# First panel's scores: left sides multiplied from SBUF, pairs made one ahead, a bar on transposes and a higher rate of handed-out work

## The chip, the cores and the metric

The kernel runs on one core of a Trainium2 chip. The metric is the device time of one execution in microseconds. The kernel before takes 3166.89 us (median of four runs, 3164.97 to 3167.02). Engines are named as in the profile: PE is TensorE (matmul), DVE is VectorE, ACT is ScalarE, POOL is GpSimd, SP is SyncE, which issues most loads. "Stage" below means the first panel's scores: from the start of their first matmul to the start of the first matmul of the next projection, both read from the matmul timeline.

## The reference

Two graph attention layers on x (2708 x 1024) and an adjacency matrix. Only the first layer's scores matter here:

```python
h = jnp.maximum(_layernorm(x, axis=-1), 0.0)
f = h @ Wf + bf
g = h @ Wg + bg
e = jax.nn.relu(f @ g.T)
scores = jnp.where(adj > 0, e, NEG)
attention = jax.nn.softmax(scores, axis=1)
```

## The kernel before

The 2708 rows are cut into five panels of columns and, on the other side, into ten pairs of row tiles and a left-over. Products use a scheme with seven products M1 to M7 per pair in place of eight. Scores of a panel are computed pair by pair, q = 0 to 9. The left sides of a pair (transposed rows and four sums of them) are made once, kept in DRAM, and read back for every panel. Pairs 0 to 4 are made in earlier stages, beside other matmuls; pairs 5 to 9 are made inside the first panel's scores.

Making a pair is a list of pieces, each with a weight in microseconds. `behind(us)` adds credit and runs pieces while there is credit; `make_until(q)` runs pieces until pair q is complete, whatever the credit:

```python
    def behind(us, psum_free=False):
        credit[0] = min(credit[0] + us, 2 * us)
        while later and credit[0] > 0 and (psum_free or not later[0][3]) and (not later[0][4] or later[0][4]()):
            credit[0] -= one()
    ...
        put_norms = lambda q: put(4.2, lambda: norms(q), lambda: fetch(q))     # normalizing: VectorE, ScalarE
        put_rows = lambda q: put(0.5, lambda: rows(q))                          # row sums: GpSimd, and stores
    ...
            if i + 1 < len(todo):
                put_norms(todo[i + 1])                    # the pair after
            put_rows(q)
            put(0.5, lambda q=q: transposes(q), takes_psum=True)   # PE, ScalarE copies
            if i > 1:
                put_dots(q)                                         # VectorE
            put(2.7 if q != LEFT else 0.0, lambda q=q: last(q))     # four sums on VectorE, stores to DRAM
```

The scores of a pair (shortened). VectorE keeps program order here (`nc.hold`), so a piece handed out at some `behind` stands in VectorE's queue at exactly that place:

```python
        for q in range(NQ):
            make_until(q + 2)
            ...
            product(q, M1, X, True);  m1 = X + rb (two additions)
            left_over()     # M4 of the pair before, its eviction, mask, maximum, and behind(rate)
            product(q, M6, Z, True);  st_lo = Z + m1;  behind(rate)
            product(q, M5, Y, True);  st_hi = Y + m1;  negate the next mask;  behind(rate)
            product(q, M2, X, False); Sa_lo = X + rb;  behind(rate)
            product(q, M7, Z, False); Sb_hi = Z + st_hi;  behind(rate)     # fifth product: needs st_lo read
            product(q, M3, Y, False); Sa_hi = Y + st_lo; mask, maximum; transposes of the next mask
            behind(2 * rate)
```

M7 accumulates into the bank that M6 left, so it can't start before VectorE has done the addition st_lo. The pool `strm` holds twelve streaming buffers (left sides, adjacency blocks, row sums and others); the pool of PSUM has eight banks.

Of the kernel before, what the change touches and what calls it, by code (L numbers as in the profile page):

```python
# [18 lines left out]
P = 128  # L19
# [38 lines left out]
def kernel(  # L58
# [19 lines left out]
    nc = InOrder(tc)  # L78
# [30 lines left out]
    NQ = len(pairs)  # L109
    pair_of = {t: (t // 2, t % 2) for t in range(MONO)}  # L110
    LEFT = NQ
# [32 lines left out]
    def bank(name, shape=(P, W), dt=FP):  # L144
        return psum.tile(list(shape), dt, tag="bank", name=name)
# [39 lines left out]
    def put(us, go, fetch=None, takes_psum=False, ready=None):  # L185
        later.append([us, fetch, go, takes_psum, ready])

    def one():
        for it in later[:2]:
            if it[1]:  # L190
                it[1]()
                it[1] = None
        us, _, go = later.pop(0)[:3]
        go()
        return us
# [5 lines that stand above are left out]
# [25 lines left out]
    def row_halves(name, from_stream=False):  # L226
        return halves(stream(name)) if from_stream else [slot(name)[:, :W] for _ in range(2)]
# [14 lines left out]
    def add(o, a, b):  # L242
        nc.vector.tensor_tensor(o, a, b, OP.add)
# [7 lines left out]
    def load_rows_of(t, o, a):  # L251

        for e in range(2):
            if t == TINY:
                nc.gpsimd.memset(o[e], 0.0)
            for ps, r in places[t]:
                load(o[e][ps], a[r:r + ps.stop - ps.start, e * W:(e + 1) * W])
# [57 lines left out]
    c0 = consts.tile([P, 1], FP, name="c0")  # L315
    r_ = consts.tile([P, NCOL], FP, name="r")
    vb = [None, None]
    made, turned_tiles = set(), set()

    def make_pairs():  # L320
        xs, hT = {}, {}

        def fetch(q):
            xs[q] = []
            for t in units[q]:
                xs[q].append(row_halves("x"))
                load_rows_of(t, xs[q][-1], x)

        def norms(q):
            for k in range(2):  # L330
                normalize(xs[q][k])

        def rows(q):
            left_h(0, *xs[q]) if q == LEFT else pair_h(0, q, *xs[q])

        def turned(q, k, e):
            t = units[q][k]
            ps = bank("h_ps", (P, NH, P))
            for c in range(NH):
                nc.tensor.transpose(ps[:, c, :], xs[q][k][e][:, c * P:(c + 1) * P], ident)  # L340
            for i, (s, n) in enumerate(pieces[0]):
                if s == t:
                    o = first_h[e].rearrange("p (c i) -> p c i", c=NH)[:, :, i * P:i * P + n]
                    nc.vector.tensor_copy(o, ps[:, :, :n])
            return ps

        def transposes(q):
            if q == LEFT:
                two = stream("hsl", (P, 2, NH, P))
                for e in range(2):  # L350
                    nc.scalar.copy(two[:, e], turned(q, 0, e))
                    nc.scalar.copy(tinyT[:, e], turned(q, 1, e)[:, :, :B32])
                store(hsl_d.rearrange("p e c j -> p (e c j)"), two.rearrange("p e c j -> p (e c j)"))
            else:
                ts = [stream("hsT", (P, 2, NH, P)) for _ in range(4)]
                hT[q] = ts, lambda i: ts[i // 2][:, i % 2]
                for k, e, i in ((0, 0, 0), (0, 1, 3), (1, 0, 7), (1, 1, 6)):
                    nc.scalar.copy(hT[q][1](i), turned(q, k, e))
            turned_tiles.update(units[q])

        def sums(q):
            if q == LEFT:
                return
            ts, i = hT.pop(q)
            at = {m: i(k) for k, m in enumerate(BY_SCORES)}
            add(at[M5], i(7), at[M4])
            sub(at[M6], at[M5], at[M1])
            sub(at[M7], at[M1], i(7))
            sub(at[M3], at[M2], at[M6])
            for g, t in enumerate(ts):  # L370
                store(hs_d[q][:, 2 * g:2 * g + 2].rearrange("p m c j -> p (m c j)"), t.rearrange("p m c j -> p (m c j)"))

        def dots(q):
            for k, t in enumerate(units[q]):
                c = col_of[t]
                dot(r_[:, c:c + 1], xs[q][k], [vb[e][:, :W] for e in range(2)], c0)
                if t == MONO:
                    nc.gpsimd.dma_start(r_[:NM, HALF:HALF + 1], r_[NM:, c:c + 1])

        def drop(q, what):  # L380
            seen.setdefault(q, set()).add(what)
            if len(seen[q]) == 2:
                xs.pop(q)

        def last(q):
            sums(q)
            drop(q, "sums")
            made.add(q)

        def bias(q):  # L390
            dots(q)
            drop(q, "dots")

        seen = {}
        put_norms = lambda q: put(4.2, lambda: norms(q), lambda: fetch(q))
        put_rows = lambda q: put(0.5, lambda: rows(q))
        put_dots = lambda q: put(3.2, lambda: bias(q), ready=lambda: vb[0] is not None)
        todo = [0, 1, LEFT] + list(range(2, NQ))
        put_norms(todo[0])
        for i, q in enumerate(todo):  # L400
            if i + 1 < len(todo):
                put_norms(todo[i + 1])
            put_rows(q)
            put(0.5, lambda q=q: transposes(q), takes_psum=True)
            if i > 1:
                put_dots(q)
            put(2.7 if q != LEFT else 0.0, lambda q=q: last(q))
            if i == 1:
                put_dots(todo[0])
                put_dots(todo[1])  # L410

    def make_until(q):
        while min(q, NQ - 1) not in made:
            one()
# [615 lines left out]
    def scores(p, B):  # L1030
# [6 lines left out]
        spread(rb, columns_of(p, r_[:, first_col[p]:]))  # L1037
        acc = slot("acc")
        S = [None] * NT
        rate = (0.6, 1.0, 0.65, 0.65, 0.65)[p]  # L1040
        lefts = {}

        def product(q, m, ps, start):
            n, i = P, BY_SCORES.index(m)
            if i % 2 == 0:
                t = stream("As", (P, 2, NH, P))
                lefts[q] = t
                k = min(2, 7 - i)
                load(t[:, :k].rearrange("p m c j -> p (m c j)"),
                     hs_d[q][:, i:i + k].rearrange("p m c j -> p (m c j)"))  # L1050
            for c in range(NH):
                nc.tensor.matmul(ps[:n, :h], lefts[q][:, i % 2, c, :n], B[m][c // 2][:, c % 2, :h],  # L1052
                                 start=(start and c == 0), stop=(c == NH - 1), skip_group_check=True)
# [12 lines left out]
        def last(q, sb, Z, m1):  # L1066

            n = P
            product(q, M4, Z, False)
            add(sb[:n, lo], Z[:n, :h], m1[:n, lo])  # L1070
            finish(q, sb, 1)
            mk_sb.pop((p, q))
            behind(rate, True)

        nc.hold = True
        left_over = None
        for q in range(NQ):
            n = P
            make_until(q + 2)
            if q + 2 <= LEFT:  # L1080
                fetch(q + 2)
            sa, sb = slot("Sa"), slot("Sb")
            S[pairs[q][0]], S[pairs[q][1]] = sa, sb
            X, Y, Z = (bank(f"s{k}") for k in "xyz")
            m1, t = slot("sm1"), slot("st")
            product(q, M1, X, True)
            for s in (lo, hi):
                add(m1[:n, s], X[:n, :h], rb[:n, s])
            if left_over:
                left_over()  # L1090
            product(q, M6, Z, True)
            add(t[:n, lo], Z[:n, :h], m1[:n, hi])
            behind(rate, True)
            product(q, M5, Y, True)
            add(t[:n, hi], Y[:n, :h], m1[:n, hi])
            if q + 1 <= LEFT:
                convert(q + 1)
            behind(rate, True)
            product(q, M2, X, False)
            add(sa[:n, lo], X[:n, :h], rb[:n, lo])  # L1100
            behind(rate, True)
            product(q, M7, Z, False)
            add(sb[:n, hi], Z[:n, :h], t[:n, hi])
            behind(rate, True)
            product(q, M3, Y, False)
            add(sa[:n, hi], Y[:n, :h], t[:n, lo])
            finish(q, sa, 0)
            if q + 1 <= LEFT:
                turn(q + 1)
            behind(2 * rate, True)  # L1110
            left_over = lambda q=q, sb=sb, Z=Z, m1=m1: last(q, sb, Z, m1)
# [358 lines left out]
```

## Time and profile before

| | before |
|---|---|
| time, median | 3166.89 us |
| span of the profiled run | 3160.3 us |
| stage (203.32 to 384.91 us) | 181.6 us |
| stage with no wait at all (worked out in the prediction) | 163.7 us |
| from the stage's end to the sums of the first aggregation (384.91 to 549.34) | 164.4 us |
| from those sums (549.34) to the end | 2611.0 us |

In what follows, "the rest" is that last part.

The view of waits, asked for the matmul engine and the stage alone (us in total, times, longest), gives for the kernel before:

```profile
PE sz L1052 <- DVE st L45: 3.2, 2, 3.0
PE sy L1052 <- DVE st L45: 3.1, 2, 1.9
PE sx L1052 <- DMA As<-hs_d: 3.1, 1, 3.1
PE mk_ps L700 <- DVE nm L45: 2.2, 1, 2.2
```

That is 11.6 us of pauses. The other 6.3 of the 17.9 us over the wait-free stage are mostly matmuls that ran slowly after a pause (3.62, 3.46, 3.29 and 4.66 us in place of 2.10, 2.10, 2.10 and 4.04), and the restarts themselves.

### The profile page before, as it was taken

The page shows a single profiled execution, that of the slowest core. Times are in us where ns is not written, and L with a number is a line of the kernel's source. Part 1 is how long each engine was busy: PE and PEld are TensorE (multiplying, and loading weights), DVE is VectorE, ACT ScalarE, POOL GpSimd, SP SyncE. Part 2 cuts the span into 40 slices and gives each one's busy share as a digit, 9 for nine tenths or more (in the row PEclk, how much of TensorE's full clock was granted, in tenths as well). Part 3 has the DMA queues.
Part 4 walks back from the last instruction along what each step waited for, and adds up shares of the span by engine and source line. Part 5 has one row for each costly group of instructions (what it writes and reads, how often), then busy time and mean ns, then how long its engine had stood idle before and what let it go on. Part 6 is the DMA issues. An engine that isn't in the chain of part 4 may idle for free.

```text
span 3160.3 us, 36134 instructions
## 1 busy us (share of the span) xinstructions
PE 3085.6 (98%) x13218; PEld 2290.2 (72%) x13218; DVE 1768.6 (56%) x3561; ACT 505.2 (16%) x872; POOL 411.8 (13%) x552
## 2 busy tenths in 40 slices
PE   8999999999999999999999999997999999999998
PEld 5577777667876688876888885864767758678684
DVE  7758576375722666327771357658574471744612
ACT  3412020010200112001020002203131130211200
POOL 3624002210002100033000101020000000100000
PEclk9999999999999999999999999998999999999999
DMA  7858749676446675467845567596655465565655
GB/s 273 317 194 297 267 136 346 197 250 212 142 126 188 221 249 172 146 196 241 274 154 152 169 206 225 199 302 208 201 177 177 153 206 151 172 194 177 212 157 196
DMA packets 273497, 650.47 MB, mean 206 GB/s; under 512 B 38160, under 2 KB 105720, under 8 KB 273320
## 3 DMA queue, kind: packets, MB, share of 16 engines
q1 hardware_dynamic: 232296, 524.04, 51.8%
q0 software_dynamic: 41024, 124.12, 11.3%
q8 instruction: 105, 1.72, 0.2%
q14 instruction: 72, 0.59, 0.1%
HBM read 535.37 MB, written 112.67 MB: 205 GB/s over the span
## 4 chain that ended last, share of the span: by engine, by line
PE 87%; issue 6%; DVE 3%; POOL 1%; DMA 1%; ACT 0%; SPq 0%; POOLq 0%; DVEq 0%; ACTq 0%
PE gy L545 12%; PE gz L545 11%; PE gx L545 11%; PE sz L1052 7%; PE pz L948 5%; PE sy L1052 5%; PE sx L1052 5%; PE gv L545 5%; PE px L948 3%; PE M_ps L465 3%; PE qz L545 3%; PE py L948 3%; PE qy L545 2%; PE qx L545 2%; PE po L921 1%
## 5 line engine op out<-in xcount | busy, mean ns | idle before, releaser
L1052 PE MATMUL sz<-B,As 128*128 128x288 f32 (+2 forms) x1200 | 296.7, 397 | 3.2 <-DVE st L45 3.2
L1052 PEld LDWEIGHTS sz<-B,As 128*128 128x128 f32 x1200 | 230.3, 193 | 51.1 <-DVE st L45 4.2
L856 POOL TENSOR_TENSOR gT<-gT,rr 128x2304 f32<-128x2304 f32 (+5 forms) x20 | 75.4, 3769 | 1088.4 <-DVE rr L45 1003.1
L1052 PE MATMUL sx<-B,As 128*128 128x288 f32 (+2 forms) x800 | 203.1, 397 | 3.2 <-DMA As<-hs_d 3.1
L1052 PE MATMUL sy<-B,As 128*128 128x288 f32 (+2 forms) x800 | 199.1, 392 | 3.1 <-DVE st L45 3.1
L545 PE MATMUL gz<-P,hc 128*128 128x288 f32 (+2 forms) x800 | 186.0, 393 | 2.3 <-ACT gT L845 2.3
L545 PE MATMUL gz<-Sa,hc 128*128 128x288 f32 (+2 forms) x800 | 186.0, 393 | 2.3 <-ACT gT L845 2.3
L545 PE MATMUL gx<-P,hc 128*128 128x288 f32 (+2 forms) x800 | 185.6, 394 | 0.0
L545 PE MATMUL gy<-T,hc 128*128 128x288 f32 (+2 forms) x800 | 184.2, 391 | 0.0
L545 PEld LDWEIGHTS gz<-Sa,hc 128*128 128x128 f32 x800 | 151.2, 190 | 36.0 <-ACT gT L845 4.4
L545 PEld LDWEIGHTS gz<-P,hc 128*128 128x128 f32 x800 | 150.9, 190 | 35.6 <-ACT gT L845 4.4
L1052 PEld LDWEIGHTS sy<-B,As 128*128 128x128 f32 x800 | 151.7, 190 | 34.2 <-DVE st L45 4.1
L545 PEld LDWEIGHTS gx<-P,hc 128*128 128x128 f32 x800 | 152.8, 191 | 32.6 <-issue 1.9
L545 PEld LDWEIGHTS gy<-T,hc 128*128 128x128 f32 x800 | 152.0, 190 | 30.5
L1052 PEld LDWEIGHTS sx<-B,As 128*128 128x128 f32 x800 | 149.1, 190 | 32.2 <-issue 3.7
L701 ACT COPY mask<-mk_ps 128x1024 bf16<-128x1024 bf16 x55 | 55.6, 1011 | 623.9 <-PE mk_ps L700 320.9
L948 PE MATMUL px<-w,gT 128*128 128x512 f32 x320 | 144.3, 603 | 6.3 <-issue 5.8
L948 PE MATMUL py<-w,ps 128*128 128x512 f32 x320 | 143.4, 598 | 0.0
L948 PE MATMUL pz<-w,ps 128*128 128x512 f32 x320 | 141.8, 593 | 0.0
L948 PEld LDWEIGHTS px<-w,gT 128*128 128x128 f32 x320 | 60.5, 192 | 82.8 <-issue 80.0
L45 DVE TENSOR_TENSOR gT<-gy,u 128x288 f32<-128x288 f32 (+2 forms) x40 | 14.8, 433 | 183.5 <-PE gy L815 183.5
L948 PEld LDWEIGHTS py<-w,ps 128*128 128x128 f32 x320 | 60.9, 192 | 76.2 <-issue 72.7
(326 smaller groups left out, 5064.6 us busy)
## 6 DMA issues: line engine op xcount, KB each, us to landing
hc<-hg_d SPq DMA_DIRECT2D x350, 512.0 KB
As<-hs_d SPq DMA_DIRECT2D x150, 512.0 KB
w<-wt_d SPq DMA_DIRECT2D x96, 512.0 KB
w<-in_L_gnn_W_dram SPq DMA_DIRECT2D x72, 512.0 KB
md<-md_d SPq DMA_DIRECT2D x56, 512.0 KB
adj_i<-in_adj_dram SPq DMA_DIRECT2D x50, 512.0 KB
hg_d<-g POOLq DMA_DIRECT2D x40, 512.0 KB, 4.8
hs_d<-hsT POOLq DMA_DIRECT2D x40, 512.0 KB, 5.4
```

The lines of the kernel that those rows point to most:

```text
L45: i = f(*a, **k)
L465: nc.tensor.matmul(ps, wfT[a][c // NH][:, c % NH, :], wgT[b][c], start=(c == 0), stop=(c == NC - 1))
L545: nc.tensor.matmul(ps[d], left(m, k, d), right(m, k), start=(start and k == 0), stop=(k == K - 1 and m not in more), skip_group_check=True)
L701: nc.scalar.copy(mk[:, :, :k4 * P], ps[:, :, :k4 * P])
L856: nc.gpsimd.tensor_tensor(of(e, s), of(e, s), by(s, k), OP.mult)
L921: nc.tensor.matmul(ps, carry[:, e, k], w_[k], start=(start and k == 0), stop=(k == NH - 1), skip_group_check=True)
L948: nc.tensor.matmul(ps, left[i][m][:, k, :], w_[k], start=(start and k == 0), stop=(k == NH - 1), skip_group_check=True)
L1052: nc.tensor.matmul(ps[:n, :h], lefts[q][:, i % 2, c, :n], B[m][c // 2][:, c % 2, :h], start=(start and c == 0), stop=(c == NH - 1), skip_g ...
```

## The change

Its intent: pairs made inside the stage need not go through DRAM for the first panel, so their left sides are multiplied straight from the tiles in SBUF; each then holds four streaming buffers, so pairs are made only one ahead; and the making is handed out between products at a higher rate.

```diff
@@ make_pairs, sums
             ts, i = hT.pop(q)
+            if in_scores[0]:
+                fresh[q] = ts
@@ make_pairs, list of pieces
-            put(0.5, lambda q=q: transposes(q), takes_psum=True)
+            put(0.5, lambda q=q: transposes(q), takes_psum=True,
+                ready=lambda q=q: not in_scores[0] or q == LEFT or q <= now[0] + 1)
@@ scores, product
-            if i % 2 == 0:
+            if q in fresh:
+                lefts[q] = fresh[q][i // 2]
+            elif i % 2 == 0:
                 t = stream("As", (P, 2, NH, P))
@@ scores, end of left_over
             mk_sb.pop((p, q))
+            fresh.pop(q, None)
             behind(rate, True)
@@ scores, loop over q
-            n = P
-            make_until(q + 2)
+            n, now[0] = P, q
+            make_until(q + 1)
+            rate = 1.7 if NQ - 1 not in made else rates[p]
```

The rates of the panels stay (0.6, 1.0, 0.65, 0.65, 0.65). Cut here is where `in_scores`, `now` and `fresh` are set up; `in_scores[0]` turns true at the start of the stage.

More of the change, by code (lines that the diff above doesn't have):

```diff
@@ L317 @@
     vb = [None, None]
+    in_scores, now = [False], [0]
     made, turned_tiles = set(), set()
+    fresh = {}
     def make_pairs():
@@ L1039, in scores @@
         S = [None] * NT
-        rate = (0.6, 1.0, 0.65, 0.65, 0.65)[p]
+        rates = (0.6, 1.0, 0.65, 0.65, 0.65)
         lefts = {}
@@ L1072, in last @@
             mk_sb.pop((p, q))
+            fresh.pop(q, None)
             behind(rate, True)
-        nc.hold = True
+        nc.hold = in_scores[0] = True
         left_over = None
         for q in range(NQ):
-            n = P
-            make_until(q + 2)
+            n, now[0] = P, q
+            make_until(q + 1)
+            rate = 1.7 if NQ - 1 not in made else rates[p]
             if q + 2 <= LEFT:
```

## The prediction

> **What bounds the kernel now.** I read the page first, then the matmul timeline of the first 700 us, then the stretches of the stage that the change touches, and last the timelines of VectorE and GpSimd in that stage.
>
> ```profile
> PE 3085.6 (98%) x13218; PEld 2290.2 (72%) x13218; DVE 1768.6 (56%) x3561; ACT 505.2 (16%) x872; POOL 411.8 (13%) x552
> ```
>
> The matmul engine is busy for 3085.6 of 3160.3 us, so all its idle time is 74.7 us, 2.4% of the span. The change removes no matmul. It can only win back idle time, and only in the first panel's scores, which the matmul timeline places at 203.3 to 384.9 us (181.6 us). Ten pairs of row tiles (q = 0 to 9) are multiplied there, seven products each, and a tail. Pairs 0 to 4 were made before; the transposes of pairs 5 to 9 stand inside the stage, at 207, 244, 280, 302 and 311 us.
>
> ```profile
> core 0: us, PE busy (x) PEld busy (x) DVE busy (x) ACT busy (x) POOL busy (x), PEclk, DMA share, GB/s
> ...
> 218.00:232.00 14.00, 14.00 (x67) 10.87 (x65) 11.11 (x25) 2.71 (x7) 2.67 (x5) 1.00 0.75 265
> ...
> 281.00:303.00 22.00, 17.85 (x83) 13.47 (x82) 20.02 (x39) 6.53 (x13) 11.16 (x14) 0.92 0.88 305
> 303.00:328.00 25.00, 19.73 (x95) 15.17 (x93) 22.21 (x43) 5.24 (x11) 11.59 (x15) 0.93 0.82 299
> ```
>
> These are the stretches of q = 1, 5 and 6. At q = 1 the matmul engine never stops and VectorE has 3 us to spare. At q = 5 and 6 VectorE is busy for 20.0 of 22 and 22.2 of 25 us: it is the bound there, and the matmul engine waits for it. The waits one by one (q = 5, then the first product of q = 7):
>
> ```profile
> 289.30 2.10 PE L1052 MATMUL sx<-B,As 128*128 128x288 f32 x8
> 294.36 3.62 PE L1052 MATMUL sz<-B,As 128*128 128x288 f32 x8 [2.96 <-DVE st L45]
> 299.17 2.21 PE L1052 MATMUL sy<-B,As 128*128 128x288 f32 x8 [1.19 <-DVE st L45]
> ...
> 327.05 3.29 PE L1052 MATMUL sx<-B,As 128*128 128x288 f32 x8 [3.08 <-DMA As<-hs_d]
> ```
>
> A product starts 1.94 us after the one before when nothing is in the way. Only one wait in the stage, 3.08 us, is for a left side read back from DRAM, which is what the change removes. The others are for VectorE's reads of the accumulators (st). To size all of it: a clean pair (q = 1) lasts from 217.52 to 231.90, 14.38 us; the five groups of transposes cost 1.75 us each where they don't wait; q = 0 lacks one product (12.44); the tail after the last pair is 13.05. So a stage without waits is 12.44 + 9 x 14.38 + 5 x 1.75 + 13.05 = 163.7 us. It takes 181.6. **All that any change here can win is 17.9 us, 0.57% of the time.**
>
> Why VectorE is late at q = 5:
>
> ```profile
> 284.39 2.61 DVE L45 TENSOR_TENSOR hsT<-hsT 128x512 f32<-128x512 f32 x4
> 286.93 0.81 DVE L45 TENSOR_TENSOR sm<-sx,rb 128x288 f32<-128x288 f32 x2
> 287.66 0.45 DVE L45 TENSOR_TENSOR Sb<-sz,sm 128x288 f32<-128x288 f32 x1
> 288.14 4.06 DVE L45 SCALAR_TENSOR_TENSOR Sb<-Sb,mask 128x576 f32<-128x576 f32 x1
> 292.24 1.70 DVE L45 TENSOR_TENSOR acc<-acc,Sb 128x576 f32<-128x576 f32 x1
> 293.86 0.45 DVE L45 TENSOR_TENSOR st<-sz,sm 128x288 f32<-128x288 f32 x1
> ```
>
> Before these lines stand the dots of the pair being made (281.19 to 284.39). Then come its four sums, then the evictions that the matmul engine wants. The mask instruction takes 4.06 us here and 0.76 us at q = 1, the maximum 1.70 against 0.76. In that very stretch GpSimd runs the four sums of the pair's rows:
>
> ```profile
> 287.86 1.28 POOL L303 TENSOR_TENSOR g<-x 128x512 f32<-128x512 f32 x1
> ```
>
> **What the Trainium skill says.** "SBUF — State Buffer", section "Who interferes with whom": a VectorE instruction with two SBUF inputs contends with a GpSimd instruction that reads SBUF, and the second to issue is blocked until the first is done. The trace agrees: the two instructions with both inputs in SBUF lost 3.3 and 0.9 us, while the additions that read PSUM kept their 0.45 us. "TensorE: Matmul & The Clock Gate", section "What's actually happening": the clock falls to half after an idle window, given as about 3.4 us. The trace shows the drop after less: after 2.96 us of idleness a product took 3.62 us instead of 2.10, after 1.95 us it did not (2.21). So a wait of about 3 us costs some 1.6 us more than itself.
>
> **The change, part by part.**
>
> Reading back. For pairs 5 to 9 four loads each are dropped: 5 x (3 x 512 + 256) KB = 9.0 MB, of 35.6 MB that moved from 203 to 330 us. It takes away the 3.08 us wait at q = 7 and the slow matmuls after it (3.29 for 2.10, and 4.66 for 4.04 us): about 5 us. The other loads stood in front of no wait.
>
> When pairs are made. This part decides, and I read it from the code rather than from the intent. Transposes of pair q + 1 are let through only once q is current; but at the start of that same q the kernel insists on pair q + 1 being complete. So transposes, dots and sums of a pair are never handed out between products: they come in one burst ahead of q's first product. At q = 0 to 3 the head of the list is the transposes of pair 5, which are barred until q = 4, so nothing is done in those four pairs, where VectorE has about 3 us or more a pair to spare (11.1 busy of 14 at q = 1 with extra work in it). Everything for five pairs then falls on q = 4 to 8. What is handed out is the normalizing and the row sums of later pairs, and with a rate of 1.7 and credit saved up to 3.4 the normalizing now goes straight after the last eviction of the pair before, one place ahead of the first st addition (at q = 5 before, it stood after that addition).
>
> VectorE's cost of a pair, from the same rows: dots 3.2 (281.19 to 284.39), sums 2.54, own evictions, masks and maxima 6.9 (0.73 + 0.45 + 1.47 + 0.37 + 0.37 + 0.80 + 3 x 0.4 + 1.47), normalizing 4.45 (294.23 to 298.66), blocking by GpSimd up to 4.25. At q = 4, 5 and 6: 3.2 + 2.54 + 6.9 + 4.45 = 17.1, with blocking 21.3, against 14.38 + 1.75 = 16.13 us of matmuls. At q = 7 there is no normalizing, at q = 8 neither that nor row sums.
>
> The path within such a pair, from the start of its transposes: dots start at 1.45 (281.19 - 279.74), sums end at 7.2, the first product's additions at 7.9, the last eviction of the pair before at 8.4, its mask and maximum at 9.9, normalizing at 14.4, the st addition at 14.8. The fifth product needs that addition and could have started at 11.5: an idle 3.35 us, hence slow, ending at 18.4; the sixth ends at 20.3; masks, and the next transposes start at 21.0. With the row sums colliding the addition ends at 19.05 and the pair takes 25.3.
> - No collision: 12.44 + 3 x 14.38 (q = 1 to 3) + 3 x 21.0 + 2 x 16.13 + 14.38 + 13.05 = 178.3 us, 3.3 less than now.
> - Collision at q = 4 to 6, and at q = 7 (20.9 us, the wait of 2.96 and its slow product, as at q = 5 now without the second wait): 12.44 + 43.14 + 75.9 + 20.9 + 16.13 + 14.38 + 13.05 = 195.9, 14.3 more.
>
> Row sums may run earlier than their place, once their inputs are normalized and buffers are free, and may then fall in VectorE's own pauses; the trace of before shows them always right behind the stores of the sums, which is where they collide. I give the collision six parts in ten: 0.4 x (-3.3) + 0.6 x 14.3 = +7.3. Since fewer read-backs leave more of the twelve streaming buffers free, partly avoided collisions are likely, so I choose +3, **3170 us**.
>
> **The rivals.**
> - The loads were the trouble, and spreading works as meant: the stage comes near 163.7 us, 3150. For it: SyncE's loads wait long for buffers, and one wait of 3.08 us shows. Against it: ten other waits name VectorE, and VectorE's work stays the same in sum and is pressed into fewer pairs.
> - VectorE becomes the bound of q = 4 to 7 altogether, at 25 us a pair, or the input of the pair two ahead (its load now stands in the burst just before its normalizing) arrives late and VectorE waits for it in order: 3181 to 3190. For it: 21.3 us of work in 16.13. Against: the loads are issued ahead by SyncE, and the row sums can move.
> - Buffers: two pairs of four tiles each are kept, with two for row sums and two for adjacency that makes all twelve. A transposed tile could wait for a product of two pairs back; the last of these is issued one product later than the transposes, so some 2 us a pair at worst, 3175 to 3180.
>
> **Range and chances.** The two sums give 3164 and 3181; with 3 to 5 us on either side for a missed slow clock or a late input: 3159 to 3183. The window of 17.9 us forbids a gain of 2% (63 us), and a loss of 63 us would need 12 us more in each of five pairs, beyond the worst sum.
>
> **What would show it.** Right: q = 0 to 3 with no transposes and 14.4 us each; the five groups of transposes at the starts of q = 4 to 8; dots and sums directly behind them on VectorE; waits of 3 to 8 us for st at the fifth product of q = 4, 5 and 6, with matmuls slowed after them; no wait for As after q = 4; no waits in q = 8. Wrong: transposes between products of an earlier pair, matmuls without pauses at q = 4 to 7, or a difference of more than 5 us after the stage.

## The result

The changed kernel takes 3184.49 us (median of four runs, 3181.78 to 3186.93) against 3166.89. Ratios here and below are the mean time of one kernel's runs over that of the other's of the same rounds, so they are not quite the ratio of the medians: 1.0057, interval 1.0039 to 1.0074. That is slower by 17.6 us, and outside the predicted range (3159 to 3183) by 1.5 us. Its class, within 2%, was right; its size was not.

The first line of the page of the changed kernel shows the span 24.5 us longer and the matmul engine busy 10 us longer with the same number of matmuls, so part of the loss is matmuls that ran slowly. (The profiled run of the changed kernel, 3186.67 us, was one of its slower runs, and that of the kernel before, 3162.18 us, was faster than all four of its timed runs. So the two spans differ by 6.9 us more than the medians, and not every difference between the two profiles belongs to the change.)

```profile
PE 3095.7 (97%) x13218; PEld 2296.9 (72%) x13218; DVE 1765.1 (55%) x3561; ACT 505.4 (16%) x872; POOL 412.4 (13%) x552
```

The timelines of both kernels, compared at the same landmarks, say where: the stage takes 200.8 us in place of 181.6 (+19.2); the part up to the sums of the first aggregation takes 169.5 in place of 164.4 (+5.1); the rest is equal to 0.1 us (2610.9 and 2611.0). The stage alone exceeds the 17.6 us between the medians. The view of waits of the stage, changed kernel:

```profile
PE sz L1059 <- DVE st L45: 25.1, 4, 7.5
PE sx L1059 <- DVE sm L45: 0.3, 1, 0.3
```

No wait for a left side is left, as intended. But four waits for the st addition now cost 25.1 us. Pauses went from 11.6 to 25.4 us (+13.8), and the other 5.4 us of the 19.2 are mostly slowed matmuls. The stretches of the stage, in the columns of the table in the prediction, pair by pair: first q = 0 to 3 together, then q = 4, 5, 6, 7 and 8:

```profile
204.00:259.00 55.00, 55.00 (x254) 42.80 (x252) 26.34 (x53) 3.54 (x6) 1.62 (x3) 1.00 0.44 138
259.00:286.00 27.00, 19.56 (x87) 14.87 (x86) 20.54 (x40) 6.79 (x13) 11.15 (x14) 0.81 0.72 247
286.00:313.00 27.00, 19.46 (x82) 14.54 (x82) 16.32 (x38) 6.58 (x12) 10.75 (x14) 0.81 0.61 218
313.00:338.50 25.50, 18.01 (x85) 13.89 (x84) 20.35 (x40) 6.79 (x13) 11.14 (x14) 0.87 0.52 190
338.50:361.00 22.50, 19.55 (x85) 14.92 (x84) 16.87 (x29) 3.28 (x7) 9.49 (x11) 0.85 0.39 153
361.00:377.00 16.00, 16.00 (x83) 12.82 (x83) 12.49 (x29) 3.05 (x7) 2.72 (x5) 1.00 0.94 287
```

For the first 55 us the matmul engine never stops and VectorE is busy for only 26.3 us: nothing of the making is done there. Then four pairs take 22 to 27 us each, with the granted clock down to 0.81, and q = 8 is clean again.

The matmul timeline at q = 4 (columns: start, duration, then the engine, the line, the tiles, the count, and in brackets the idle time before it and what ended it):

```profile
268.75 2.10 PE L1059 MATMUL sx<-B,As 128*128 128x288 f32 x8
278.29 4.21 PE L1059 MATMUL sz<-B,As 128*128 128x288 f32 x8 [7.44 <-DVE st L45]
282.29 3.08 PE L1059 MATMUL sy<-B,As 128*128 128x288 f32 x8
...
353.12 4.21 PE L1059 MATMUL sz<-B,hsT 128*128 128x288 f32 x8 [2.95 <-DVE st L45]
```

The fifth product waits 7.44 us, and then it and the sixth take 4.21 and 3.08 in place of 2.10 each. The last line is q = 7, with hsT (the tiles in SBUF) as the left side. VectorE in the same stretch of q = 4, and what GpSimd was doing:

```profile
267.66 4.05 DVE L45 SCALAR_TENSOR_TENSOR Sb<-Sb,mask 128x576 f32<-128x576 f32 x1
271.75 1.70 DVE L45 TENSOR_TENSOR acc<-acc,Sb 128x576 f32<-128x576 f32 x1
273.38 1.27 DVE L45 BATCH_NORM_STATS2 bn<-x 128x6 f32<-128x512 f32 x2
...
277.79 0.45 DVE L45 TENSOR_TENSOR st<-sz,sm 128x288 f32<-128x288 f32 x1
```

```profile
267.37 1.28 POOL L303 TENSOR_TENSOR g<-x 128x512 f32<-128x512 f32 x1
```

The mask instruction and the maximum are blocked by GpSimd's row sums, as at q = 5 of the kernel before; and the normalizing (273.38 to 277.79) now stands before the st addition, where before it stood behind it.

At q = 5 the same length of wait came about in another way. In the built program the product M4 of pair 4, whose left side is the last one read back from DRAM, stands three products later than in the other pairs:

```profile
294.01 2.21 PE L1059 MATMUL sx<-B,hsT 128*128 128x288 f32 x8 [0.32 <-DVE sm L45]
296.06 2.10 PE L1059 MATMUL sz<-B,As 128*128 128x288 f32 x8
305.38 4.21 PE L1059 MATMUL sz<-B,hsT 128*128 128x288 f32 x8 [7.22 <-DVE st L45]
```

```profile
298.20 0.46 DVE L45 TENSOR_TENSOR Sb<-sz,sm 128x288 f32<-128x288 f32 x1 [4.24 <-PE sz L1059]
```

VectorE, in order, stood idle for 4.24 us until that product had ended. So there GpSimd's row sums fell into an idle time and blocked little (the mask instruction took 1.06 us), but the st addition came just as late.

The 5.1 us after the stage come from one place in the first aggregation. The matmul timeline, kernel before, then changed kernel:

```profile
503.73 2.21 PE L811 MATMUL gx<-Sa,hl 128*128 128x288 f32 x8 [2.31 <-DMA hl<-hgl_d]
...
507.10 19.67 PE L545 MATMUL gz<-Sa,hc 128*128 128x288 f32 x80 [0.47 <-ACT gT L845]
```

```profile
524.07 4.21 PE L816 MATMUL gx<-Sa,hl 128*128 128x288 f32 x8 [3.52 <-DMA hl<-hgl_d]
...
530.02 21.33 PE L550 MATMUL gz<-Sa,hc 128*128 128x288 f32 x80 [0.47 <-ACT gT L850]
```

A wait for a transfer that was there before grew by 1.2 us, and this time the matmuls after it were slowed (4.21 for 2.21, 21.33 for 19.67). Of the fourteen kernels profiled, this part took 164.0 to 164.9 us in seven and 166.7 to 169.5 us in seven. Six of these last have the change's bar on transposes, and of the kernels with the bar only one is among the short ones. In the seven long ones the wait shown first here lasted 2.7 to 3.5 us and slowed the matmuls after it, in the others at most 2.3 us. So the later making of the pairs goes together with the long form more often than not; but each kernel was profiled once, and which transfer passes a delay on was not tried apart. Nor can the times settle it: the timed runs of the kernel before are 2.8 to 4.8 us slower than its profiled run, so they may hold the long form too. How much of the 5.1 us the change causes is not shown.

### The profile page after: what moved, and what is told of

Read it like the earlier page. It is cut to its first block, busy times and chain, and to the rows that moved or that the text cites. A ratio compares the mean times of both kernels' runs of the same rounds, so it can differ in the third digit from the quotient of the medians.

```text
span 3184.8 us, 36093 instructions
## 1 busy us (share of the span) xinstructions
PE 3095.7 (97%) x13218; PEld 2296.9 (72%) x13218; DVE 1765.1 (55%) x3561; ACT 505.4 (16%) x872; POOL 412.4 (13%) x552
## 3 DMA queue, kind: packets, MB, share of 16 engines
q0 software_dynamic: 41024, 124.12, 11.2%
## 4 chain that ended last, share of the span: by engine, by line
PE 80%; issue 5%; DVE 4%; DMA 1%; POOL 1%; ACT 0%; SPq 0%; POOLq 0%; DVEq 0%; ACTq 0%
PE gz L550 11%; PE gy L550 11%; PE gx L550 11%; PE sz L1059 7%; PE pz L953 5%; PE gv L550 5%; PE sy L1059 4%; PE sx L1059 4%; PE px L953 3%; PE py L953 3%; PE qz L550 3%; PE qy L550 2%; PE qx L550 2%; PE po L926 1%; PE mk_ps L705 1%
## 5 line engine op out<-in xcount | busy, mean ns | idle before, releaser
L1059 PE MATMUL sz<-B,As 128*128 128x256 f32 (+2 forms) x1080 | 264.3, 394 | 7.4 <-DVE st L45 7.4
L1059 PEld LDWEIGHTS sz<-B,As 128*128 128x128 f32 x1080 | 206.5, 192 | 47.9 <-DVE st L45 7.9
L1059 PE MATMUL sx<-B,As 128*128 128x256 f32 (+2 forms) x720 | 180.7, 394 | 0.0
L1059 PE MATMUL sy<-B,As 128*128 128x256 f32 (+2 forms) x720 | 178.8, 391 | 0.0
L1059 PEld LDWEIGHTS sy<-B,As 128*128 128x128 f32 x720 | 137.6, 191 | 26.9
L1059 PEld LDWEIGHTS sx<-B,As 128*128 128x128 f32 x720 | 133.8, 190 | 24.5
```

The source lines that it names most:

```text
L1059: nc.tensor.matmul(ps[:n, :h], lefts[q][:, i % 2, c, :n], B[m][c // 2][:, c % 2, :h], start=(start and c == 0), stop=(c == NH - 1), skip_g ...
```

## The experiments

The theory: the loss comes from when and where the pairs are made. The bar empties q = 0 to 3 and forces a burst ahead of q = 4 to 8; the normalizing stands one place too early; GpSimd's row sums block VectorE. The rivals: the tiles kept in SBUF cost buffers; VectorE's total alone counts; transfers take over. Each kernel was timed in five rounds against the kernel before on one chip (three chips in all); all results were correct.

**Nothing multiplied from SBUF.**

```diff
             ts, i = hT.pop(q)
-            if in_scores[0]:
-                fresh[q] = ts
```

> The changed kernel, but pairs made in the stage are read back from DRAM again (nothing is multiplied from SBUF); one ahead, the bar on transposes and the rate 1.7 stay. Theory (the loss comes from WHEN the pairs are made: nothing at q = 0 to 3, everything at q = 4 to 8, with VectorE as the bound): 3180 to 3188 us, as the changed kernel, with waits of 7 us for st at the fifth product of q = 4 and 6. Rival (the left sides kept in SBUF take the streaming buffers, so the tiles kept are what costs): back to 3165 to 3172.

Measured: 3183.81 us (3181.76 to 3185.77), ratio to before 1.0059. The stage takes 200.3 us against 200.8. What gave the change its name costs nothing and gains nothing: there are the four waits for st again (7.44, 7.43, 7.37, 2.95 us), now with one wait for a left side at q = 8 (1.57 us). The wait at q = 4:

```profile
279.01 3.74 PE L1057 MATMUL sz<-B,As 128*128 128x288 f32 x8 [7.44 <-DVE st L45]
```

The rival falls.

**Only pair q insisted on at the start of q.**

```diff
-            make_until(q + 1)
+            make_until(q)
```

> The changed kernel, but at the start of q only pair q itself is insisted on, so that transposes, dots and sums of pair q + 1 can be handed out between the products of q. Theory: the fifth product no longer waits 7 us behind dots, sums and normalizing in one go, but VectorE still has 21 us of work against 16 us of matmuls at q = 4 to 6 and q = 0 to 3 stay empty: 3165 to 3174 us, a gain of 10 to 19 on the changed kernel. Rival (the burst costs nothing of its own, only VectorE's total counts): no better than 3180.

Measured: 3163.87 us (3162.57 to 3168.51), ratio 1.0001; a gain of 18 to 21 us on the changed kernel (by ratios and by medians), with a time 1.1 us below the expected range. The stage takes 179.6 us. Now the transposes come after the first handing-out of q, dots before the st addition, sums and normalizing behind it; the longest wait of the matmul engine in the stage is 1.95 us:

```profile
297.80 0.23 PE L710 MATMUL mk_ps<-identb,nmt 64*128 64x64 bf16 x2 [1.95 <-DVE nmt L45]
```

VectorE runs the same 248 instructions in the stage of both kernels (128.6 us here, 125.7 in the changed kernel), and the making still lies in q = 4 to 8, so the burst had a cost of its own, and VectorE's total is not what sets the time. This kernel keeps every idea of the change, and it is level with the kernel before.

**Spread from q = 0 on, at a lower rate.**

```diff
-            if in_scores[0]:
-                fresh[q] = ts
...
-            put(0.5, lambda q=q: transposes(q), takes_psum=True,
-                ready=lambda q=q: not in_scores[0] or q == LEFT or q <= now[0] + 1)
+            put(0.5, lambda q=q: transposes(q), takes_psum=True)
...
-            rate = 1.7 if NQ - 1 not in made else rates[p]
+            rate = 0.8 if NQ - 1 not in made else rates[p]
```

> The changed kernel without the bar and without left sides from SBUF, rate 0.8 instead of 1.7: the making of pairs 5 to 9 is spread over q = 0 to 8. Theory: VectorE then has about 13.4 us of work a pair against 14.4 to 16.1 of matmuls, most waits go, stage 165 to 172 us, 3150 to 3158 in all, faster than both kernels. Rival (reading back from DRAM or the transfers are what makes the matmul engine wait): 3167 or more, with waits for As.

Measured: 3167.97 us (3167.33 to 3171.2), ratio 1.0011, stage 186.1 us. A miss, and the time is the rival's (3167 or more); but of 13.6 us of waits in the stage only 3.0 are for left sides, the other 10.6 for VectorE. The average load of VectorE fits into a pair, but the pieces don't. Normalizing (4.45 us in one piece) still landed in front of the st addition, and blocked instructions (3.4 to 4.6 us) ahead of it. The wait at q = 3:

```profile
266.32 4.21 PE L1056 MATMUL sz<-B,As 128*128 128x288 f32 x8 [4.74 <-DVE st L45]
```

**Row sums on VectorE.**

```diff
-        on = nc.vector if l else nc.gpsimd
+        on = nc.vector
```

> The changed kernel with the four sums of a pair's rows on VectorE instead of GpSimd. Theory (they block VectorE's two-input instructions for 3.3 to 4.3 us at q = 4, 6 and 7): the mask instruction falls from 4.06 to 0.76 us, VectorE has 2.5 us of sums more but after the st addition, so the wait of the fifth product falls from 7.4 to about 3 us and the time to 3172 to 3180. Rival (the blocking is only shown, VectorE's own work is what counts): 2.5 us more in each of four pairs, 3190 to 3196.

Measured: 3170.75 us (3168.9 to 3171.83), ratio 1.0017, stage 185.7 us: a gain of 13 us on the changed kernel, more than the theory gave. The wait at q = 4 is 3.20 us in place of 7.44, at q = 7 1.24 in place of 2.95. Doing 2.5 us more on VectorE is cheaper than being blocked for 4.25 us at the wrong place. The wait at q = 5, which had another cause, stayed (6.92 us), as it should.

**No handing-out after the last eviction of the pair before.**

```diff
             fresh.pop(q, None)
-            behind(rate, True)
```

> The changed kernel without the one handing-out that stands right after the last eviction of the pair before, so that normalizing goes one place later, behind the first st addition (as it stood before the change). Theory (that one place is why the fifth product waits 7.4 us and not 3.0): waits of some 3.0 and 1.2 us instead of 7.4 at q = 4 and 6, and 22 us a pair instead of 25 to 27: 3169 to 3176 us. Rival (VectorE's total alone sets the length of a pair, the order is without weight): 3181 or more.

Measured: 3164.08 us (3161.48 to 3168.27), ratio 0.9991. The waits at the fifth product fell as expected (3.0 us at q = 4, 2.95 at q = 6). The time is better than expected, and the trace says why: the edit reached all panels. The stage takes 189.1 us, 11.7 less than in the changed kernel, which is the theory's size; and the rest after the first aggregation takes 2603.6 us in place of 2610.9. There another view of waits changed. The matmul engine from 400 us on, changed kernel, then this one:

```profile
PE mk_ps L705 <- DVE nm L45: 7.4, 6, 3.8
```

```profile
PE mk_ps L705 <- DVE nm L45: 1.2, 2, 0.8
```

In the later panels, too, work handed out at this place had made the negated mask late, with a wait of up to 3.8 us and slowed matmuls behind it. This has nothing to do with the change; it was there before it.

**The same in the first panel alone.**

```diff
-            behind(rate, True)
+            if p:
+                behind(rate, True)
```

> The changed kernel without the handing-out after the last eviction of the pair before, this time in the first panel alone (the run that dropped it in all panels also gained some 7 us in the later panels, beside 11.7 in the first panel's scores). Theory: only the first panel's scores shorten, by 11 to 12 us, and the later panels keep their waits of 3.8 us for the negated mask: 3170 to 3175 us. Rival (the gain of that run was the place of normalizing alone): 3163 to 3167.

Measured: 3175.7 us (3173.3 to 3178.38), ratio 1.0032, stage 190.5 us. The stage gains 10.3 us and the rest stays at 2610.9. The median is 0.7 us above the expected range. One place in the queue is worth about 10 us of the stage.

**The kernel before with row sums on VectorE** (the same edit as above, in the other kernel).

> The kernel before the change, with the four sums of a pair's rows on VectorE. Theory (the blocking by GpSimd makes the 2.96 us waits at q = 5 and 6 with the slowed products after them): those waits go or fall under 1 us, VectorE has 2.5 us more a pair: 3158 to 3164 us. Rival (the 2.5 us more cost as much as the blocking): 3165 or more.

Measured: 3159.94 us (3155.79 to 3160.84), ratio 0.9978, stage 176.5 us, 5.1 less than before. The waits at the fifth product are gone; one of 2.58 us at the sixth and one for a left side (3.83 us) have come up in their place.

**No bar.** (The first experiment, and:)

```diff
-            put(0.5, lambda q=q: transposes(q), takes_psum=True,
-                ready=lambda q=q: not in_scores[0] or q == LEFT or q <= now[0] + 1)
+            put(0.5, lambda q=q: transposes(q), takes_psum=True)
```

> The changed kernel without left sides from SBUF and without the bar on transposes; the rate stays 1.7. Beside the kernel that differs from it by the bar alone (3184) it shows what the bar costs. Theory (the bar both empties q = 0 to 3 and forces transposes, dots and sums into one burst ahead of the first product): the pairs are made from q = 0 on, between products, still one a pair: 3163 to 3172 us. Rival (the bar only moves the same load from early to late pairs): 3180 or more.

Measured: 3171.58 us (3169.69 to 3172.51), ratio 1.0016, stage 189.5 us against 200.3 in the first experiment, which differs by the bar alone. The bar costs 10.8 us of the stage. What is left are ten waits of up to 3.4 us between 215 and 300 us of the span, six of them for VectorE and three for left sides: by these waits, making one pair in every pair is still too dense. The bar can't simply be taken from a kernel that multiplies from SBUF: neither the kernel before with SBUF left sides and no bar nor the changed kernel without its bar can be built; the build stops with a deadlock at the release of a streaming buffer. So whether SBUF left sides would help a well spread making stays open.

**At the ends of pairs only.**

```diff
-            rate = 1.7 if NQ - 1 not in made else rates[p]
+            making = NQ - 1 not in made
+            rate = 0.0 if making else rates[p]
-            behind(2 * rate, True)          # after M3
+            behind(6.3 if making else 2 * rate, True)
-        put_rows = lambda q: put(0.5, ...   # and: no bar, no SBUF left sides, row sums on VectorE
+        put_rows = lambda q: put(2.7, ...
```

> No left sides from SBUF, no bar, row sums on VectorE, and while pairs are being made work is handed out at the end of each pair alone, 6.3 us by the kernel's own weights, from q = 0 on. Theory (what matters is that no pair gets more on VectorE than it can do before the fifth product asks for the st addition; dots and sums, 5.7 us, made no wait at q = 8 of the changed kernel): nearly no waits for VectorE, stage 164 to 170 us, 3148 to 3156 us, faster than both. Rival (buffers or late read-backs stop the matmul engine once VectorE does not): 3160 or more, with waits for As.

Measured: 3166.85 us (3164.94 to 3170.01), ratio 1.0003, stage 189.0 us. A miss, by my own edit: there are six groups of transposes in the stage, most likely since the larger weight had slowed the making in the stages before it, and two pairs' pieces piled up twice:

```profile
312.33 4.21 PE L1056 MATMUL sx<-B,As 128*128 128x288 f32 x8 [4.87 <-DVE sm L45]
...
336.67 4.21 PE L1056 MATMUL sx<-B,As 128*128 128x288 f32 x8 [5.28 <-DVE sm L45]
```

**The same, mended.** Weight 0.5 again, 5.6 a pair, credit set to zero at the start of the stage, and in the later panels no handing-out after the last eviction.

> As the run that hands out at the ends of pairs alone (3166.9 us), mended: its larger weight for row sums had pushed the making of a sixth pair into the stage and piled two pairs' pieces on q = 6 and 7 (waits of 4.9 and 5.3 us). Here 5.6 us a pair from an empty credit, the old weight, and the later panels without the handing-out after the last eviction. Theory: dots and sums (5.7 us) and normalizing and row sums (7.0 us) take turns, waits for VectorE stay under 1.5 us each, stage 166 to 172 us: 3146 to 3153 us. Rival (read-backs of just stored left sides set the pace then): 3156 or more, with waits for As.

Measured: 3152.09 us (3151.74 to 3155.45), ratio 0.9961 (0.9948 to 0.9973), stage 178.7 us, the rest 2603.1. The time lies in the expected range, but the stage is 7 us longer than expected (166 to 172), so the range of the whole was right by luck. For VectorE the matmul engine waits once, 0.93 us. The rival has come true instead: 11.2 us in four waits for left sides, such as this one:

```profile
288.83 2.18 PE L1056 MATMUL sx<-B,As 128*128 128x288 f32 x8 [3.44 <-DMA As<-hs_d]
```

**The kernel before with both repairs.** Row sums on VectorE, and in the later panels no handing-out after the last eviction.

```diff
-        on = nc.vector if l else nc.gpsimd
+        on = nc.vector
             mk_sb.pop((p, q))
-            behind(rate, True)
+            if p == 0:
+                behind(rate, True)
```

> The kernel before the change with the row sums on VectorE and, in the panels after the first, without the handing-out after the last eviction of the pair before. Theory: the two gains (6.3 us and 7 us) lie in different stages and add: 3151 to 3156 us. Rival (one of them hides the other or was the clock): 3158 or more.

Measured: 3151.16 us (3148.68 to 3152.63), ratio 0.9954 (0.9941 to 0.9966). The two gains add: stage 176.9, the rest 2603.3. This and the run before can't be told apart, and both beat both kernels.

**The changed kernel with both repairs.**

> The changed kernel with its left sides from SBUF, repaired in two places: row sums on VectorE and no handing-out after the last eviction of the pair before, in any panel. Theory: VectorE has 19.6 us a pair at q = 4 to 6 and the waits are short enough to keep the clock: stage 174 to 182 us, 3148 to 3157 us. Rival (with everything at q = 4 to 8 the stage can't be shorter than in the kernel before): 3160 or more.

Measured: 3163.19 us (3160.17 to 3167.73), ratio 0.9991, stage 189.0 us. A miss: the rest gained its 7 us (2604.1), the stage was no shorter than with one repair (185.7 or 189.1). In its built program the order of matmuls is another one: at q = 4 the transposes of the next mask stand ahead of the fifth and sixth products,

```profile
275.04 1.03 PE L705 MATMUL mk_ps<-identb,nm 128*128 128x128 bf16 x8 [4.16 <-DVE nm L45]
```

and wait for the negated mask, which stands behind the normalizing on VectorE; the next pair then waits 5.20 us more. Why the order came out so was not tried apart.

Side by side, the stage of the kernels that differ from another by one thing (us; the differences overlap, so they don't add up; one profiled run of each kernel):

| kept from the changed kernel, except | stage | against |
|---|---|---|
| left sides from SBUF | 200.3 | 200.8 |
| ... and the bar | 189.5 | 200.3 |
| insisting on pair q + 1 | 179.6 | 200.8 |
| row sums on GpSimd | 185.7 | 200.8 |
| the one place of normalizing | 190.5 | 200.8 |

## Why the prediction was wrong, and where it was right

The bound and the mechanism held; the ceiling was not put to the test, since no run came near a stage of 163.7 us (the shortest took 176.5). As forecast, q = 1 to 3 stayed empty at 14.4 us each, and q = 0 at 12.4 (the forecast wrote 14.4 for it too, against its own sum); the five groups of transposes stand at the starts of q = 4 to 8 (259.2, 285.9, 313.1, 338.5 and 360.9 us); no wait for a left side remained in the stage; the waits at the fifth product of q = 4 to 6 are 7.2 to 7.5 us; q = 8 took 16.08 us against 16.13 predicted. Removing the bar, the forced pair, the place of normalizing and GpSimd's row sums one at a time gained 10 to 21 us of the stage each, so these steps are shown, not only argued. The reading from code that "making the pairs one ahead, handed out between products" would not be handed out at all decided the sign, and it was right.

What failed is the step from two sums to a number: the discount on the collision, and the cost of a slowed clock after a wait.

First, "I give the collision six parts in ten ... partly avoided collisions are likely, so I choose +3". The collision came at q = 4, 6 and 7, right behind the stores of the sums. The trace of before had shown it every time: all four sets of row sums in the stage blocked VectorE there, by 3.5 to 4.3 us (three sets stood behind the stores of the sums, the one at 235.66 us behind those of normalized rows). At q = 5 it was avoided, and a late product of the pair before cost the same (7.22 us). There was no evidence for giving avoidance four parts in ten; the freer streaming buffers that the forecast named as a reason changed nothing (first experiment). The sum with collisions, 195.9 us for the stage, was the prediction that the profile supported.

Second, the term "a wait of about 3 us costs some 1.6 us more than itself". After three of the four waits the fifth product took 4.21 and the sixth 3.1 to 3.2 us in place of 2.10 each, which is 3.1 us; only after the one at q = 6 was it 1.7 (3.77 for 2.10). In three pairs that is 1.5 us each. With it and with some 0.5 us at q = 5 (the wait of 0.32 us and its longer restart), the worst sum becomes 200.9, and 200.8 was measured. That it fits so closely is partly luck, since at q = 5 the wait had another cause.

Third, the range. Its text allows 3 to 5 us on either side of 3164 and 3181, which would reach to 3184 or 3186; the upper end was written as 3183.

The signs that the forecast gave of being wrong were "transposes between products of an earlier pair", which did not happen, "matmuls without pauses", which did not either, and more than 5 us after the stage. The profiles show 5.1 us there, in the first aggregation; but as said under the result, they do not show that the change causes it, and the forecast had no term for it. Whether it also makes part of the run-to-run spread of the changed kernel, 3181.8 to 3186.9 us, is not shown.

Smaller slips: the estimate that removing the wait for left sides was worth "about 5 us" is not visible anywhere, since with the pairs read back again (first experiment) the stage was as long; "ten other waits name VectorE" was a miscount, as the view of waits of the stage shows five; and of these one, of 2.19 us, is for the negated mask, not for st. The 9.0 MB of dropped loads were set against what moved from 203 to 330 us, but the loads of the last pairs are issued from 328.9 us on.

Of the rivals, the first (transfers were the trouble) is refuted for this change by the first experiment, but it is true of the next step: once VectorE is out of the way, waits for left sides of 2.2 to 3.4 us set in (the mended run). The second (VectorE the bound of q = 4 to 7 altogether, 3181 to 3190) named the measured time, but not by its mechanism: VectorE was busy for only 16.3 to 20.5 of 22.5 to 27 us in these pairs, and the run with only pair q insisted on does the same work in a stage 21 us shorter. No normalizing waited for its input either. The third, buffers, may show in one place: the load of the last left side of pair 4 was issued at 279.2 us, after SyncE had waited 7.4 us for VectorE's negation of a mask. Whether that is why the built program has the product late at q = 5 was not tried apart; the matmul engine did not wait for that load. It cost little on balance, for with the pairs read back (first experiment) that pair took 26.3 us by collision in place of 27.2.

## What to carry to other kernels

When work is handed out behind matmuls on an engine that keeps program order, ask for each place what the matmul engine needs next from that engine, and put the longest piece right behind that, not ahead of it: one place was worth 10 us here. Read the guard and the force on a list together: a piece that may not run before q and must be done when q starts is never handed out at all. And if the profile shows a collision every time, predict with it.

## What the Trainium skill lacked or had wrong

- "TensorE: Matmul & The Clock Gate", section "What's actually happening", gives an idle window of about 3.4 us before the clock falls and as long a busy time before it rises, and says that the window runs free. The runs make the first no threshold, which fits the last: matmuls were slowed after a wait of 2.38 us (line below) and not after waits of 3.44 and 3.18 us, all three in one execution (the mended run). Estimated by doubling what was lost, since the slowest products took twice their time (4.21 for 2.10), the slowed stretch lasted 3.3 us at q = 6 of the changed kernel (twice the 1.66 us that the fifth product's turn grew by, 3.60 for 1.94) and 6.1 us at q = 4 (4.00 + 2.92 us of turns for 3.88, so 3.04 us lost, doubled). In the first aggregation of the changed kernel 4.2 us were lost after a wait of 3.52 us (2.00 + 0.57 + 1.66, the matmuls after it against those of the kernel before). So the cost of a pause was anything from nothing to 4.2 us on top, and the page would help with such a range.

```profile
252.97 3.82 PE L1056 MATMUL sx<-B,As 128*128 128x288 f32 x8 [2.38 <-DMA As<-hs_d]
```

- "SBUF — State Buffer", section "Who interferes with whom", agrees with the blocked instructions told here. It could say what it costs when GpSimd runs several such instructions in a row: at q = 5 of the kernel before four of them, 5.5 us together, took 4.25 us from VectorE (3.3 and 0.95 us), not one instruction's length: VectorE's mask instruction, begun at 288.14 us, ended only after the third of them had (291.57). The same section says that `tensor_scalar` can contend though it has one input: in the run with only pair q insisted on, the negation of a mask remainder took 4.08 us in place of 0.28 beside GpSimd's row sums, four times.
- No page gives a size for the blocking that a two-input sum on GpSimd brings: moving a pair's four sums of 128x512 from GpSimd (1.28 us each) to VectorE (0.68 us each) shortened the kernel before by 6.3 us, 5.1 of them in the stage.
